# A gated quantized MLP: conditioning by VectorE, another order of the first slots, and five steps in other places

## The chip, the core and the metric

One core of a Trainium2 chip runs the kernel. Its engines work side by side, each through its own list of instructions in order, and wait for each other by semaphores: TensorE (PE in the profile, its weight loads PEld), VectorE (DVE), ScalarE (ACT), GpSimd (POOL) and SyncE (SP), which here issues nearly all transfers between memory and the on-chip buffers. The metric is the device time of one execution in microseconds, the median of several.

## The reference

x is (4, 1024, 512): four batches of 1024 tokens. Each batch has a row of 128 conditioning values, which scales the 512 channels after an RMS norm. Then comes a gated product with 2048 values and 2048 gates, an exact GELU, and a product down to 512 with both sides quantized: 8 bits for each token, three levels for the weights.

```python
scale = cond @ norm_w.T + 1.0
ms = jnp.mean(x * x, axis=-1, keepdims=True)
h = x * (scale[:, None, :] * jax.lax.rsqrt(ms + EPS))
u = h @ up_w.T
val, gate = jnp.split(u, 2, axis=-1)
h = val * jax.nn.gelu(gate, approximate=False)
hq = act_quant(h)          # round(h * 127 / max|h|) of each token, scaled back
wq = weight_quant(down_w)  # -1, 0, 1 by the mean of |w|
y = hq @ wq.T + x
```

## The kernel before

**Slots.** The 2048 values and gates are cut into 16 tiles of 128, and each batch into two halves of 512 tokens. One tile for one batch is a *slot*; g counts slots over all batches (slot 16 is the first of the second batch), j within a batch. A float32 number is carried as two 16-bit parts, a *high* and a *low* one, so each product has three terms: low by high, high by low, high by high.

**The first batch** (`first_batch` and the straight code above it) is computed plainly: `plain_half(j, h)` makes, for tile j and half h, 12 matmuls for the gate (`pg`), a Gelu on ACT, 12 matmuls for the value (`pv`) and a DVE operation that multiplies them into H. Meanwhile the up weights are prepared: `w_load` (SP), `w_range` (DVE finds each row's power of two), `w_scale` (POOL), `w_turn` (PE turns the tile), `w_high` (ACT casts the high part), `w_low` (DVE the rest), `w_evac` (ACT copies the turned tile), `s_sums` (POOL makes sums of quarters), `s_high` (ACT), `s_low` (POOL) and `s_spill` (SP writes them to memory). The later batches load these sums and need 7 products of 6 matmuls for a slot instead of 8 (`product`, `slot`).

**Conditioning.** norm_w is loaded first on SP (L157), then x. PE turns cond and norm_w (`cond_prep`), multiplies them (`cond_scale`, L172), and the largest value of each batch gives a power of two that is spread over all partitions (`cond_largest`, `cond_range`). `first_high` and `first_low` multiply the turned x of batch 0 by scT while they cast it. For the other batches `cond_rows` multiplies all rows out, each 32 times, and writes them to `rows_dram`; `cond_load_scale` fetches one (`sc`) with four transfers, and `cond_bring` (L217) scales it on DVE.

**Down weights.** `d_load`, then `d_sum` on ACT for the absolute values, `d_total` (DVE, L350, makes `wpart`) and `d_mean` (PE's `pmean`, L355, and two DVE operations), all in slot 5; `d_round` and `d_put` prepare wd. ACT's `d_sum` writes into a buffer that DVE's largest values (`pair_max`, tile gm) also use.

**Order.** The program order of each engine is written out by hand. Pools of buffers make a writer wait for the last reader; of PSUM banks A and E have two, B one, po three. In the later batches a slot's steps have places x, y and z: `plan` gives the four token tiles of the next batch their places for load, norm, scale, high, low and turn; the rest is filled in by cost.

**The end.** The last batch has no slot behind it. Eight tiles of the batch before (`old_tile`) run on PE while DVE and ACT quantize the last batch (`work`), `per` steps of work between two tiles; `ends` holds the evacuations of tiles that still wait for it. Then come the last products (`po_end`), whose banks the old tiles hold.

Of the kernel before, what the change touches and what calls it, by code (L numbers as in the profile page):

```python
# [41 lines left out]
def glu_quant_kernel(  # L42
# [22 lines left out]
    G = P // B  # L65
# [37 lines left out]
    rows_dram = tc.dram_tile([P, D], F32, name="rows_dram")  # L103
# [42 lines left out]
    condT = cpool.tile([P, B], F32, name="condT")  # L146
# [4 lines left out]
    nwT = R[:, 1, 512:1024]  # L151
    cg = R[:, 1, 1024:1152].rearrange("p (b o) -> p b o", b=B)
    junk = R[:, 1, 2048:4096].rearrange("p (n d) -> p n d", d=D)
    cn = sm.tile([B, C], F32, name="cn", bufs=1)

    def cond_load():
        SP.dma_start(out=nw, in_=norm_w.rearrange("(k p) c -> p k c", p=P))  # L157
        ACT.dma_start(out=cn, in_=cond)

    def cond_prep():  # L160
        pc = bank("E", 2, [P, B], "pc")
        PE.transpose(pc, cn, ident[:B, :B])
        DVE.tensor_copy(condT, pc)
        pt = bank("E", 2, [P, D], "pt")
        for k in range(NK):
            PE.transpose(pt[:, k * P : (k + 1) * P], nw[:, k, :], ident)
        ACT.copy(nwT, pt)

    def cond_scale():
        pq = bank("A", 2, [P, NK, B], "pq")  # L170
        for k in range(NK):
            PE.matmul(pq[:, k, :], nwT[:, k * P : (k + 1) * P], condT, start=True, stop=True)  # L172
        DVE.tensor_scalar(scT, pq, 1.0, None, ALU.add)

    def cond_largest():
        mx = sm.tile([P, B], F32, name="mx", bufs=1)
        DVE.tensor_reduce(
            mx, scT.rearrange("p k b -> p b k"), AX.X, ALU.max, apply_absolute_value=True
        )
        pm = bank("A", 2, [B, P], "pm")  # L180
        PE.transpose(pm, mx, ident)
        return pm

    def cond_range(pm):
        d4 = sm.tile([B, 1], F32, name="d4", bufs=1)
        DVE.tensor_reduce(d4, pm, AX.X, ALU.max)
        DVE.tensor_scalar(d4, d4, 1e-30, None, ALU.max)
        pow2_floor(d4)
        dg = sm.tile([B, B], F32, name="dg", bufs=1)
        DVE.tensor_scalar(dg, ident[:B, :B], d4, 1.0 / X_UP, ALU.mult, ALU.mult)  # L190
        pd = bank("A", 2, [P, B], "pd")
        PE.matmul(pd, ones[:B, :], dg, start=True, stop=True)
        DVE.tensor_copy(dx, pd)
    def cond_bring_first():
        DVE.reciprocal(ux, dx)
        DVE.tensor_scalar(scT[:, :, 0], scT[:, :, 0], ux[:, 0:1], None, ALU.mult)

    def cond_rows():

        pq = bank("A", 2, name="pq_rows")  # L200
        PE.matmul(pq, cg.rearrange("p b o -> p (b o)"), nwT, start=True, stop=True)
        rows = junk[:, 0]
        DVE.tensor_scalar(rows, pq, 1.0, None, ALU.add)
        SP.dma_start(out=rows_dram, in_=rows)

    def cond_groups():
        DVE.tensor_copy(cg, condT.rearrange("p (b o) -> p b o", o=1).to_broadcast([P, B, G]))

    def cond_load_scale(b):

        sc = wpool.tile([P, D], F32, name=f"sc_{b}", tag="sc", bufs=1)
        for n in range(P // G):
            SP.dma_start(out=sc[n * G : (n + 1) * G, :], in_=rows_dram[b * G : (b + 1) * G, :])
        return sc
# [15 lines left out]
    def wf(j):  # L230

        return H[:, 15 + j % 2].rearrange("p t (n f) -> p (t n) f", n=2)
# [3 lines left out]
    def w_load(j):  # L236
        for t in (1, 0):
            SP.dma_start(out=wn(j)[:, t], in_=up_v[j][:, t])
# [254 lines left out]
    def h_half(g, h):  # L493
        return h_slots(g)[:, 0, h]
# [13 lines left out]

    live = {}

    def slot(g, x=nothing, y=nothing, z=nothing, middle=nothing, late=nothing):

        up = g < B * NJ
        prev = live.pop(g - 1, None)
        if up:
            cur = live[g] = {}
            cur["A"] = bank("A", 2, name=f"A_{g}")
            product(0, g, cur["A"], True, True)
            pb = bank("B", 1, name=f"B_{g}")
            ACT.copy(pb, cur["A"])  # L520
            cur["E"] = bank("E", 2, name=f"E_{g}")
            product(4, g, cur["E"], True, True)
            cur["v"] = wpool.tile([P, TOK], F32, name=f"v_{g}", tag="v")
            ACT.copy(cur["v"], cur["E"])  # L524
            product(1, g, pb, False, True)
            cur["t1"] = wpool.tile([P, TOK], F32, name=f"t1_{g}", tag="t1")
            ACT.activation(cur["t1"], pb, AF.Gelu, scale=gain(g, 1))  # L527
# [6 lines left out]
        if up:  # L534
            product(5, g, cur["A"], False, True)
            cur["t2"] = wpool.tile([P, TOK], F32, name=f"t2_{g}", tag="t2")
            ACT.copy(cur["t2"], cur["A"])  # L537
# [122 lines left out]
    DVE.memset(eps, EPS)  # L660
    ACT.activation(start_t, one, AF.Sqrt)
# [13 lines left out]
    def first_sums(n):  # L675
        ACT.activation(junk[:, n % 4], X0[:, n], AF.Square, accum_out=ssq0[:, n : n + 1])
        DVE.scalar_tensor_tensor(
            junk[:, (n + 1) % 4], X0[:, n + 1], 1.0, X0[:, n + 1], ALU.mult, ALU.mult,
            accum_out=ssq0[:, n + 1 : n + 2],
        )  # L680

    def rsqrt_start(t, y):

        z = sm.tile([P, NA], F32, name="newton", bufs=1)
        ACT.activation(z, t, AF.Sqrt, scale=1.0 / D, bias=eps)
        DVE.tensor_scalar(t, t, 1.0 / D, EPS, ALU.mult, ALU.add)
        DVE.reciprocal(y, z)
        DVE.tensor_tensor(z, y, y, ALU.mult)
        DVE.scalar_tensor_tensor(z, z, -0.5, t, ALU.mult, ALU.mult)
        DVE.scalar_tensor_tensor(y, z, 1.5, y, ALU.add, ALU.mult)  # L690
# [17 lines left out]
    def first_low(h, k, pt):  # L708
        c = slice(h * TOK, (h + 1) * TOK)
        DVE.scalar_tensor_tensor(  # L710
            XP[:, 1, k, c], pt, scT[:, k, 0:1], XP[:, 0, k, c], ALU.mult, ALU.subtract
        )
# [7 lines left out]
    cond_load()  # L720
    first_load(0)
    first_load(2)
    w_load(0)
    first_load(4)
    w_load(1)
    first_load(6)
    w_load(2)
    keep_warm(6)
    cond_prep()
    for n in (0, 2):  # L730
        first_sums(n)
    rsqrt_start(ssq0[:, 0:4], rs0[:, 0:4])
    cond_scale()
    keep_warm(3)
    pm = cond_largest()
    first_scale(0, ACT)
    first_scale(1, DVE)
    first_scale(2, ACT)
    first_scale(3, ACT)
    ptx = [po_bank(f"ptx_0_{k}") for k in range(3)] + [bank("A", 2, name="ptx_0_3")]  # L740
    first_turn(0, ptx)
    first_turn(1, ptx)
    w_range(0, 1, 2)
    w_scale(0, (1,), ACT)
    cond_range(pm)
    first_turn(2, ptx)
    first_turn(3, ptx)
    w_turn(0, [bank("E", 2, name=f"pw_0_{t}") for t in (1, 0)], (1,))
    cond_bring_first()
    first_high(0, 0, ptx[0])  # L750
# [4 lines left out]
    first_low(0, 0, ptx[0])  # L755
    w_low(0, (1,))
    for k in range(1, NK):
        first_high(0, k, ptx[k])
        first_low(0, k, ptx[k])
    w_turn(0, ts=(0,))  # L760
    w_high(0, (0,))
    w_evac(0)
    w_low(0, (0,))
    ACT.activation(start_t, neghalf[:, 0:1], AF.Gelu)
    w_range(1)
    w_gain(1)
    cond_groups()
    w_scale(1)
    for n in (4, 6):
        first_sums(n)  # L770
    rsqrt(ssq0[:, 4:8], rs0[:, 4:8])
    plain_half(0, 0)
    w_turn(1)
    w_high(1)
    w_evac(1)
    w_low(1)
    for n in range(4, 8):
        first_scale(n, ACT if n % 2 else POOL)
    w_load(3)
    w_range(2)  # L780
    w_gain(2)
    w_scale(2)
    plain_half(1, 0)
    ptx = [po_bank(f"ptx_1_{k}") for k in range(3)] + [bank("A", 2, name="ptx_1_3")]
    for n in range(NA, 2 * NA):
        first_turn(n, ptx)
    for k in range(NK):
        first_high(1, k, ptx[k])
        first_low(1, k, ptx[k])
    s_sums(0)  # L790
    w_load(4)
    w_range(3)
    w_gain(3)
    w_scale(3)
    plain_half(0, 1)
    w_turn(2)
    w_high(2)
    w_low(2)
    w_range(4)
    w_gain(4)  # L800
    s_high(0)
    s_low(0, POOL)
    s_spill(0)
    w_evac(2)
    s_sums(1)
# [13 lines left out]
    def first_batch(j, sc):  # L819
# [23 lines left out]
        if j == 5:  # L843
            d_mean(part)
# [13 lines left out]
        plain_half(j, 1)  # L858
        for i, h in pairs[2:]:
            for f in pair_max(0, i, h):  # L860
                f()
# [18 lines left out]

    for n in D_LOAD[0] + D_LOAD[1]:
        d_load(n)
    w_load(5)
    cond_rows()
    plain_half(1, 1)
    s_high(1)
    s_low(1, POOL)
    s_spill(1)
    w_turn(3)
    w_high(3)  # L890
    w_low(3)
    w_evac(3)
    w_scale(4)
    s_sums(2)
    s_high(2)
    s_low(2, POOL)
    s_spill(2)
    for n in D_SUM[1]:
        d_sum(n)
    for j in range(2, NJ):  # L900
        if j == 4:
            sc = cond_load_scale(1)
            cond_bring(1, sc)
        first_batch(j, sc if j >= 4 else None)
# [72 lines left out]
    for b in range(1, B):  # L977
# [18 lines left out]
        if b + 1 < B:  # L996
# [8 lines left out]
                (p0 + 2, p0 + 4, ((9, "z"), (12, "x"), (12, "y"), (13, "z"), (14, "x"), (14, "y"))),  # L1005
# [130 lines left out]
    per = -(-len(work) // (2 * NA - 3))  # L1136
# [12 lines left out]
    for f in ends[:1] + work + ends[1:]:  # L1149
        f()  # L1150
# [48 lines left out]
```

## Time and profile before

| | |
|---|---|
| runs | 765.2 us median of three, 761.91 to 765.37 |
| profiled execution | 766.27 us; span from first to last instruction 764.5 us |
| granted clock | 0.997 |
| 0 to 5 us, 5 to 10 us | PE busy 3.57 and 3.58, transfers 161 and 342 GB/s |
| 50 to 60, 60 to 70 us | transfer share 0.99 and 1.01 |
| 100 to 150, 150 to 200 us | PE 50.00 and 50.00, DVE 44.11 and 41.11, POOL 36.98 and 43.07 |
| sc from rows_dram | four issues 71.81 to 74.86, used on DVE at 78.92 |
| dq from am_dram, 1024 single elements | 4.2 to 4.4 us from issue to landing |

Busy times are sums over an engine's instructions; PE's are pipelined and their ends modelled, so a busy PE is not one at its peak. A wait is put down to the engine whose semaphore came last. Idle time costs only where it delays the chain that ends last.

### The profile page before, as it was taken

What the parts mean: (1) busy time and instruction counts of PE and PEld (TensorE: products, weight loads), DVE (VectorE), ACT (ScalarE), POOL (GpSimd) and SP (SyncE); (2) the same over time, 40 slices, a digit from 0 to 9 for tenths busy, and PEclk for the clock granted to TensorE, in tenths of its full rate; (3) what the DMA queues carried; (4) which work ended last, traced back from release to release, by engine and by line L of the source; (5) the groups of instructions that cost most, each with busy time, mean ns of one, the idle gap of its engine ahead of it and who ended that gap; (6) DMA issues with size and microseconds to landing.
All of it is one profiled execution on the core that took longest, in us unless ns stands there. A gap on an engine that the chain in (4) does not pass through costs nothing.

```text
span 764.5 us, 9577 instructions
## 1 busy us (share of the span) xinstructions
PE 744.8 (97%) x3485; PEld 347.6 (45%) x3485; DVE 544.0 (71%) x781; ACT 376.0 (49%) x614; POOL 199.4 (26%) x221
## 2 busy tenths in 40 slices
PE   7899899999999999999999999999999999999997
PEld 4454445545444444444444444444444444444443
DVE  5746769988879886544679886554679887445895
ACT  4558445566234656353434666444333665332263
POOL 0478547989310030333010020243020000000100
PEclk9999999999999999999999999999999999999999
DMA  6159355778823325366833334557732333333153
GB/s 224 38 187 380 108 172 150 196 191 194 232 90 115 116 81 174 136 185 180 193 110 102 112 117 136 175 154 202 179 119 97 97 102 112 115 106 110 51 185 110
DMA packets 92784, 111.54 MB, mean 146 GB/s; under 512 B 59961, under 2 KB 60477, under 8 KB 92738
## 3 DMA queue, kind: packets, MB, share of 16 engines
q1 hardware_dynamic: 92730, 110.94, 47.8%
q8 instruction: 27, 0.44, 0.2%
q14 instruction: 19, 0.16, 0.1%
q10 hardware_dynamic: 8, 0.00, 0.0%
HBM read 74.47 MB, written 23.35 MB: 128 GB/s over the span
## 4 chain that ended last, share of the span: by engine, by line
PE 87%; DMA 3%; DVE 3%; ACT 2%; SPq 1%; issue 1%; POOL 1%; DVEq 0%; ACTq 0%; POOLq 0%
PE A L464 32%; PE E L464 16%; PE po L646 10%; PE B L464 8%; PE pv L479 8%; PE pg L479 8%; PE po_end L646 3%; PE pw L267 1%; DMA s_dram<-SXY 1%; DMA H<-in_x_dram 1%; PE ptx L702 1%; DVE gm L565 1%; DMA sc<-rows_dram 1%; DMA R<-in_x_dram 1%; DVE R L567 1%
## 5 line engine op out<-in xcount | busy, mean ns | idle before, releaser
L464 PEld LDWEIGHTS <-SXY 128*128 128x128 f16 x2016 | 197.2, 98 | 241.8 <-issue 4.2
L464 PE MATMUL A<-R,SXY 128*128 128x512 f16 x1152 | 264.6, 379 | 1.0 <-ACT t L537 1.0
L464 PE MATMUL E<-R,SXY 128*128 128x512 f16 x576 | 140.0, 379 | 0.0
L530 DVE SCALAR_TENSOR_TENSOR H<-A,sg,t 128x512 f32<-128x512 f32 x48 | 36.0, 750 | 83.5 <-PE A L464 83.5
L543 ACT ACTIVATE t<-t,sg 128x512 f32<-128x512 f32 x48 | 34.5, 720 | 106.5 <-DVE t L542 106.5
L646 PE MATMUL po<-wd,R 128*128 128x512 bf16 x384 | 85.3, 379 | 0.0
L646 PEld LDWEIGHTS <-R 128*128 128x128 bf16 x512 | 50.1, 98 | 61.5 <-issue 1.2
L620 DVE TENSOR_TENSOR H<-H,am 128x1024 f32<-128x1024 f32 x64 | 76.3, 1217 | 0.0
L581 POOL PARTITION_ALL_REDUCE am<-R x8 | 14.6, 1819 | 223.7 <-DVE R L567 223.7
L464 PE MATMUL B<-R,SXY 128*128 128x512 f16 x288 | 70.0, 379 | 2.4 <-ACT B L520 2.4
L565 DVE TENSOR_REDUCE gm<-H 128x512 f32<-128x1024 f32 x56 | 69.0, 1233 | 2.6 <-DMA wd<-tn 1.6
L542 DVE TENSOR_TENSOR t<-E,t 128x512 f32<-128x512 f32 x48 | 32.6, 680 | 49.4 <-PE E L464 49.4
L479 PE MATMUL pg<-R,SXY 128*128 128x512 f16 x264 | 61.7, 379 | 3.0 <-ACT R L706 1.7
L479 PE MATMUL pv<-R 128*128 128x512 f16 x252 | 63.2, 379 | 0.0
L373 POOL TENSOR_TENSOR rs<-ssq,neghalf 128x2 f32<-128x2 f32 (+1 forms) x13 | 9.6, 738 | 205.5 <-DVE ssq L372 205.2
L479 PEld LDWEIGHTS <-SXY 128*128 128x128 f16 x396 | 38.6, 98 | 49.2 <-issue 3.6
L479 PEld LDWEIGHTS <-R 128*128 128x128 f16 x372 | 36.6, 99 | 43.4 <-issue 1.0
L527 ACT ACTIVATE t<-B,sg 128x512 f32<-128x512 f32 x48 | 33.0, 687 | 38.8 <-PE B L464 37.0
L537 ACT COPY t<-A 128x512 f32<-128x512 f32 x48 | 28.0, 583 | 47.8 <-PE A L464 47.7
L628 ACT ACTIVATE H<-H 128x1024 f32<-128x1024 f32 x39 | 40.9, 1049 | 20.9 <-DVE H L620 20.9
L567 DVE TENSOR_TENSOR R<-R,gm 128x512 f32<-128x512 f32 x56 | 42.9, 766 | 1.4
L524 ACT COPY v<-E 128x512 f32<-128x512 f32 x48 | 28.1, 585 | 31.2 <-PE E L464 26.9
(154 smaller groups left out, 884.9 us busy)
## 6 DMA issues: line engine op xcount, KB each, us to landing
SXY<-s_dram SPq DMA_DIRECT2D x48, 640.0 KB, 4.0
SXY<-s_dram SPq DMA_DIRECT2D x48, 256.0 KB, 4.3
s_dram<-SXY SPq DMA_DIRECT2D x11, 896.0 KB, 4.0
H<-in_L_cond_up_w_dram SPq DMA_DIRECT2D x32, 256.0 KB, 4.3
xr<-in_x_dram SPq DMA_DIRECT2D x19, 256.0 KB, 4.7
out_dram<-xr SPq DMA_DIRECT2D x19, 256.0 KB, 2.2
s_dram<-R SPq DMA_DIRECT2D x5, 896.0 KB, 4.7
H<-in_x_dram SPq DMA_DIRECT2D x8, 512.0 KB, 5.8
```

Source lines behind the costliest of these rows:

```text
L464: PE.matmul(o, s[:, w, k, :], tv[:, :, c, l, k, :], start=start and n == 0, stop=stop and n == len(TERMS) - 1, skip_group_check=True,)
L479: PE.matmul(ps, a[k // 2][:, w, k % 2, :], XP[:, l, k, h * TOK : (h + 1) * TOK], start=n == 0, stop=n == len(terms) - 1,)
L524: ACT.copy(cur["v"], cur["E"])
L527: ACT.activation(cur["t1"], pb, AF.Gelu, scale=gain(g, 1))
L530: DVE.scalar_tensor_tensor(h_half(g - 1, 0), prev["A"], gain(g - 1, 0), prev["t1"], ALU.mult, ALU.mult)
L542: DVE.tensor_tensor(prev["t2"], prev["E"], prev["t2"], ALU.add)
L543: ACT.activation(prev["t2"], prev["t2"], AF.Gelu, scale=gain(g - 1, 1))
L565: DVE.tensor_reduce(gm[0], v, AX.X, ALU.max, apply_absolute_value=True)
L567: return [largest, lambda: DVE.tensor_tensor(m, m, gm[0], ALU.max)]
L620: DVE.tensor_tensor(v, v, r.to_broadcast([P, 2, TOK]), ALU.mult)
L628: ACT.activation(v, v, AF.Copy, bias=MAGIC)
L646: PE.matmul(po, q[:, h, j, a * P : (a + 1) * P], wd[:, j, :], start=j == 0, stop=j == NJ - 1,)
```

## The change

The conditioning is computed by DVE: products of norm_w with the broadcast row of cond, summed along the row (`cond_scale` for batch 0, `cond_scale_rest` for the others later). norm_w and cond come over ACT's queue, x first on SP. The range and spread are computed once for batch 0 and once for batches 1 to 3. `cond_rows` writes the three rows from scT, one element for each partition and group, in slot 3; `cond_load_scale` broadcasts a row with one transfer. The start works by tiles of x: the first sums and the Newton steps for two tiles at a time, twelve warming matmuls first, more of them between.

Slots 0 to 2 run on the first 512 tokens; then the second half of x is turned, and the slots run on the second half. `plain_first` is tile 0 with its terms in another order, and the turning of weights between them.

Five steps stand elsewhere: `d_mean` behind the second half of slot 5; in slot 16 the sixth product and its copy ahead of the second product (`first_value`); token 3's high, low and turn one place later each; three steps of work between old tiles; the last work behind all evacuations.

```diff
-    def cond_load():
-        SP.dma_start(out=nw, in_=norm_w.rearrange("(k p) c -> p k c", p=P))
-        ACT.dma_start(out=cn, in_=cond)
...
+    def cond_load(b0, b1):
+
+        v = cond[b0:b1].rearrange("b c -> (b c)").partition_broadcast(P)
+        ACT.dma_start(out=cb[:, b0:b1].rearrange("p b c -> p (b c)"), in_=v)
+
+    def cond_scale(b):
         for k in range(NK):
-            PE.matmul(pq[:, k, :], nwT[:, k * P : (k + 1) * P], condT, start=True, stop=True)
-        DVE.tensor_scalar(scT, pq, 1.0, None, ALU.add)
+            DVE.scalar_tensor_tensor(
+                dots, nw[:, k], 1.0, cb[:, b], ALU.mult, ALU.mult, accum_out=scT[:, k, b : b + 1]
+            )
+
+    def cond_scale_rest():
...
+        DVE.tensor_tensor(v, w, s, ALU.mult)
+        DVE.tensor_reduce(scT[:, :, 1:].rearrange("p k b -> p b k"), v, AX.X, ALU.add)
...
     def cond_rows():
 
-        pq = bank("A", 2, name="pq_rows")
-        PE.matmul(pq, cg.rearrange("p b o -> p (b o)"), nwT, start=True, stop=True)
-        rows = junk[:, 0]
-        DVE.tensor_scalar(rows, pq, 1.0, None, ALU.add)
-        SP.dma_start(out=rows_dram, in_=rows)
+        for b in range(1, B):
+            SP.dma_start(out=rows_dram[b].rearrange("(k p) -> p k", p=P), in_=scT[:, :, b])
...
         sc = wpool.tile([P, D], F32, name=f"sc_{b}", tag="sc", bufs=1)
-        for n in range(P // G):
-            SP.dma_start(out=sc[n * G : (n + 1) * G, :], in_=rows_dram[b * G : (b + 1) * G, :])
+        SP.dma_start(out=sc, in_=rows_dram[b].partition_broadcast(P))
...
+    def plain_first(between):
+
+        ps = {1: bank("B", 1, name="pg_0_0"), 0: bank("A", 2, name="pv_0_0")}
+        gate, a21, a22 = a_parts(0)
+        for n, (t, w, l) in enumerate(
+            ((1, 0, 0), (1, 1, 0), (0, 0, 0), (0, 1, 0), (1, 0, 1), (0, 0, 1))
+        ):
+            if n in between:
+                between[n]()
...
+        def first_value():
+            product(5, g, cur["A"], False, True)
+            cur["t2"] = wpool.tile([P, TOK], F32, name=f"t2_{g}", tag="t2")
+            ACT.copy(cur["t2"], cur["A"])
...
             ACT.copy(cur["v"], cur["E"])
+            if not prev:
+                first_value()
             product(1, g, pb, False, True)
...
-    cond_load()
     first_load(0)
+    w_load(0, (1,))
     first_load(2)
-    w_load(0)
+    w_load(0, (0,))
+    w_load(1)
     first_load(4)
-    w_load(1)
     first_load(6)
     w_load(2)
-    keep_warm(6)
...
+    keep_warm(12)
+    first_sum(0)
+    first_sum(1)
+    cond_scale(0)
+    mx = cond_largest(0, 1)
+    pm = cond_over(mx, 0, 1, "A")
+    rsqrt_start(ssq0[:, 0:2], rs0[:, 0:2])
     keep_warm(3)
-    pm = cond_largest()
+    pd = cond_spread(cond_range(pm, 0, 1), 0, 1, "A")
+    keep_warm(1)
+    first_sum(2)
     first_scale(0, ACT)
+    first_sum(3)
+    w_range(0, 1, 2)
     first_scale(1, DVE)
+    rsqrt_start(ssq0[:, 2:4], rs0[:, 2:4])
+    w_scale(0, (1,), ACT)
     first_scale(2, ACT)
+    cond_undo(pd, 0, 1)
+    cond_bring_first()
+    first_scale(3, DVE)
...
     first_turn(0, ptx)
+    keep_warm(2)
     first_turn(1, ptx)
...
-        if j == 5:
-            d_mean(part)
+        if j == 3:
+            pd = cond_spread(dg, 1, B, "po")
+            cond_undo(pd, 1, B)
+            cond_rows()
...
         plain_half(j, 1)
+        if j == 5:
+            d_mean(part)
...
+    plain_first({1: second_part, 4: second_slot})
+    w_load(3)
...
+    plain_half(1, 0, third_slot)
...
+    plain_half(2, 0, other_half)
+    w_load(5)
+    w_scale(3)
+    s_all(0)
+    s_sums(1)
...
+    cond_scale_rest()
+    mx = cond_largest(1, B)
+    plain_half(0, 1)
+    s_all(1)
+    s_sums(2)
...
+    w_scale(4)
+    plain_half(1, 1)
...
-    for j in range(2, NJ):
+    for j in range(3, NJ):
...
-                (p0 + 2, p0 + 4, ((9, "z"), (12, "x"), (12, "y"), (13, "z"), (14, "x"), (14, "y"))),
+                (p0 + 2, p0 + 4, ((9, "z"), (12, "x"), (12, "y"), (14, "x"), (14, "y"), (14, "z"))),
...
-    per = -(-len(work) // (2 * NA - 3))
+    per = 3
...
-    for f in ends[:1] + work + ends[1:]:
+    for f in ends + work:
         f()
```

## The prediction

> **What bounds the kernel now.** I read the busy row and the chain of waits first: PE is busy for 97% of the span and holds 87% of the chain, so only time in which PE stands, or runs at half its clock, can be won. The list of PE's waits then says where, and the timelines say why. The first 100 us (first rows) and the rest of the span:
>
> ```profile
> PE 744.8 (97%) x3485; PEld 347.6 (45%) x3485; DVE 544.0 (71%) x781; ACT 376.0 (49%) x614; POOL 199.4 (26%) x221
> ...
> PE pmean L355 <- DVE wpart L350: 3.5, 1, 3.5
> PE pm L181 <- DVE mx L177: 1.9, 1, 1.9
> PE pg L479 <- ACT R L706: 1.7, 7, 0.4
> ...
> PE pw L267 <- POOL H L259: 1.1, 2, 0.7
> PE pg L479 <- DVE SXY L289: 1.1, 1, 1.1
> ...
> PE B L464 <- ACT B L520: 2.4, 2, 1.2
> PE A L464 <- ACT t L537: 1.0, 1, 1.0
> ...
> PE po_end L646 <- DVE SXY L653: 0.9, 1, 0.9
> ```
>
> Columns: who waits for whom; us in total, times, longest. Next, rows of the timelines of PE, DVE and ACT (start, length, engine, line, in brackets the idle time before and who ended it) and, between them, the row 90 to 100 of the table by stage, whose last three numbers are granted clock, transfer share and GB/s:
>
> ```profile
> 17.34 0.39 PE L479 MATMUL pg<-R,SXY 128*128 128x512 f16 x1 [0.24 <-ACT SXY L280]
> ...
> 78.92 0.49 DVE L217 TENSOR_SCALAR sc<-sc,ux 128x512 f32<-128x512 f32 x1 [6.19 <-DMA sc<-rows_dram]
> ...
> 91.38 0.42 PE L355 MATMUL pmean<-wpart,one 128*128 128x1 f32 x2 [3.45 <-DVE wpart L350]
> 91.66 1.95 PE L267 MATMUL pw<-ident,H 128*128 128x128 f32 x8
> ...
> 90.00:100.00 10.00, 8.62 (x38) 4.85 (x39) 3.72 (x13) 4.23 (x9) 6.40 (x8) 0.83 0.51 167
> ...
> 215.09 0.69 ACT L527 ACTIVATE t<-B,sg 128x512 f32<-128x512 f32 x1 [1.78 <-DVE sg L488]
> 216.30 2.75 PE L464 MATMUL A<-R,SXY 128*128 128x512 f16 x12 [1.02 <-ACT t L537]
> 364.61 1.85 ACT L443 CAST H<-H 128x512 f16<-128x512 f32 x3
> 366.37 0.57 ACT L520 COPY B<-A 128x512 f32<-128x512 f32 x1
> ```
>
> The reader sees five places: a start in which the first real matmul stands at 17.34; a chopped stretch up to 60.12, where the sixth half slot ends; a stand of 3.45 us at 88 to 91, after which the granted clock of ten microseconds is 0.83 (1.7 us lost; the same eight transposes take 1.95 us there and 1.04 elsewhere); three single waits in batches 1 and 2; one at the end.
>
> **Pace of PE.** A half slot is 24 matmuls: the rows that start at 54.94 and 60.12 give 5.18. Eight transposes take 0.87 (48.01 to 48.89). From 17.34 to 60.12 are 42.78 us; the work in it is 6 x 5.18 + 4 x 0.87 (w_turn) + 1.75 (16 turns of x, at 32.48) + 0.86 (the product for the rows, 41.97 to 42.83) = 37.2, so 5.6 are lost.
>
> **The start, step by step.** Gone: the transposes of the conditioning, its four products, the ACT copy; x no longer queues behind norm_w. Before, the first pair of x tiles was issued at 1.23 and its sums began at 7.29. Now it is issued half a microsecond earlier, but norm_w shares the same transfer engines from ACT's queue: between 6.3 and 7.3, I take 6.8. The second pair has half a weight tile ahead of it (256 KB at about 0.37 MB/us is 0.7 us): 8.9, instead of 8.7. ACT now takes both first sums (2 x 0.72), and Sqrt 0.3: 8.6. DVE's four dot products of 128 elements have no row; between 0.18 (the smallest operations) and 0.69 (512 elements), I take 0.4 with the accumulator read, so 1.6, and 0.4 to add one and take the largest: done at 9.0. Then in DVE's order, by the rows of before: Newton 0.87, range of the conditioning 0.87, range of the gate weights 1.16, scale of tile 1 0.48, second Newton 0.87, spread undone 0.55, scale of tile 3 0.48. That is 9.0 + 5.3 = 14.3, with DVE never idle. A trap is here: the fourth bank of the first turn is the one that holds the spread factor, so PE's first turn ends only when DVE has copied it (13.3); 2 warming matmuls, three turns and the gate weights' turn follow, 2.2 us at full clock. ACT's first high part then runs at 15.5 and **the first matmul at 16.1**, 1.2 earlier than now.
>
> Here a rule decides a size. The Trainium skill, "TensorE: Matmul & The Clock Gate", section "Part 1: The HAM clock gate", says the clock is doubled after one busy window of about 3.4 us, which runs free of the program, and halved after one idle window. The rows show the halving (3.45 us idle, then 0.83). They show the early state by spacing: the six warming matmuls take 2.74 us for what later takes 1.46, so the first 16 us are at half clock. Twelve in place of six, 0.43 apart, are busy for 5.2 us, which holds a whole window in (5.2 - 3.4)/3.4, about half, of all phases, a little more if a nearly full one counts; three, one and two more keep the later windows from being idle. By the rule the clock is full at 13 us, by the row (half until 16) the same turns cost 2.2 more and the first matmuls too. I take full clock, and keep the other as a rival.
>
> **Slots 0 to 2.** The load of the other three conditioning rows costs ACT half a microsecond of issue ahead of the value weights' cast, which DVE does not yet wait for. PE now has three half slots of other weights before it needs the second half of x. Still lost: 1.1 us for the first four matmuls, each behind an ACT high part (0.58 apart against 0.22). The other waits go, since weights and sums come a half slot sooner; but POOL becomes late: its sums (2.8 per slot) and low parts (2.25) stand ahead of the scaling of tile 4. PE ends (2,0) at 16.1 + 3 x 5.18 + 5 x 0.43 + 1.75 + 1.1 = 36.7 and wants tile 4 two halves and a w_turn later, at 47.9; POOL gets the first s_high at 37.1 and needs 2.25 + 2.8 + 2.25 + 2.8 + 1.36: 48.5. So 0.6 is lost. PE's work is 37.2 - 0.86 + 0.43 (half of the first turn, now after the first matmul) = 36.8, and the sixth half ends at 16.1 + 36.8 + 1.1 + 0.6 = 54.6: **5.5 won** with the start. DVE's new product and sum for the other three batches (1536 elements; 1.22 per 1024 by L620, so 3.6 for both) and 0.4 more lie beside the matmuls of half slot (0,1); without that cover they would delay only the release of a bank that has another half slot's time. The two small matmuls for the three batches cost PE 0.2.
>
> **d_mean half a slot later.** It moves past 12 + 12 matmuls and one w_turn on PE (6.05 us), and its two DVE operations behind w_low and one evacuation; behind them on DVE stands only d_round, first needed at 100. wpart is late because DVE stood 6.19 for sc, then worked 12.2 us to wpart. If DVE comes no earlier, PE reaches it 2.6 us after wpart. **3.45 + 1.7 = 5.15 won**, if sc comes no later. sc: its four issues took 3.05 us of SP and are one now. But the rows are written only in slot 3, as 3 x 512 single elements, and sc waits on SP for the first of them, behind the spill of slot 4. The skill, "DMA: Bandwidth & Descriptors", section "Rules for kernel authors", says a strided last dimension becomes one descriptor per element and should be rearranged: 1536 descriptors against 128. The nearest row is dq, 1024 single elements, which lands in 4.3 us, no more than larger transfers. The skill's rule says avoid, the row says 4 to 5 us, once. I take the row. On SP the rows now stand behind four spills and the loads up to slot 7; POOL's pace lets SP issue them near 61, sc at about 66 behind the spill, landed at 70.5. PE ends (4,0) at 71 and (5,1) at 88 (54.6 + 5.2 per half and 0.9 per w_turn). DVE has wpart 12.2 after sc, 83. Slack 5 us. Bounds: nothing lost, or, were each element 0.2 us, 96 per transfer engine, 19 us.
>
> **Single moves.** In slot 16 first_value goes ahead of the Gelu that waits for sg behind pair maxima: the ACT copy of A no longer stands behind it. 1.0 won. Token 3's high part (1.85 on ACT) leaves 13 z, where it stood ahead of the copy of B, for 14 x, behind the Gelu and ahead of a copy that is due 1.8 us later; its low follows on DVE at the same point of the slot as now, its transpose is SP's next issue as now (372.6), 10 us before the batch that reads it: 2 x 1.2 = 2.4 won. At the end three steps between old tiles in place of five let DVE evacuate tile 5 (733.3) seven steps sooner; DVE is full to 752 either way, and PE's last products need its pieces later than they come: 0.9 won, 0 if DVE's order holds up something I don't see.
>
> **Sum.** 5.5 + 5.15 + 1.0 + 2.4 + 0.9 - 0.2 = 14.8. The profiled execution took 766.27 (span 764.5): 751.5. The median shown is 765.2, one microsecond below it, which I don't take off.
>
> **Rivals.** (1) *The start gives nothing*: the clock is half until about 17, x or the dot products come a microsecond late; the sixth half ends 3.4 to 5.4 later than 54.6, as now or little better, and the rest holds: 755 to 757, say 755.5. For it: DVE is a closed chain from 9 to 25 us, so each late step passes on. Against: the waits for POOL and DVE in slots 1 and 2 are gone from the order itself, whatever the first matmul's time. (2) *Only the moves that are named work and sc comes late*: with 8 us more, DVE frees the bank of (4,0) at 81.7, when PE wants it at 79.6, and is a little behind at d_mean too: 2 to 4 us and perhaps the clock, 754 to 757. For it: transfers were saturated at 50 to 70 us (share 0.99 to 1.01). (3) *Slower*: single-element writes to memory at 0.2 us or more each: with 0.25, sc is 24 us late and DVE stands for it, the weight range and the evacuation of (4,0) queued behind; PE stands 18 us for that bank in slot 5 and loses 1.7 of clock: 771.5. It decides from about 0.2 us per element. Against it: dq's 4.3 us. (4) *No change*: DVE or POOL, with less idle time, hands the waits back in slots 6 to 15. Against: there PE stands not at all between 100 and 210, and DVE waited for PE for 8 us.
>
> **Chances.** Likeliest 0.60 (its own range 748 to 755); (1) 0.23; (2) 0.06; (3) and other losses 0.07; (4) 0.04. Range 747.5 to 758.5. 0.5% (3.8 us) is about what a measurement here tells from none. Faster 0.89, within 0.04, slower 0.07.
>
> **What would show it.** First matmul near 16 and sixth half near 54.6; no wait for wpart, and granted clock 1.00 from 90 to 100; waits for t at slot 16 and for B gone; DVE's wait for sc under 5 us. Wrong if a wait for sc, for scaled weights or for a transposed tile of the next batch appears in PE's list with more than 2 us, or a clock below 1.00 past 20 us.

## The result, and the profile after

The changed kernel takes 762.28 us (median of 20 runs, 759.69 to 764.5) where the kernel before, beside it, takes 764.99 (median of 20): ratio 0.9966, 95% interval 0.9954 to 0.9978, or 2.7 us less. 14.8 were forecast. The profiled execution took 763.18, with a span of 761.4. In its list of PE's waits (who waits for whom; us in total, times, longest), whole:

```profile
PE pm L185 <- DVE mx L178: 4.0, 1, 4.0
PE pv L485 <- DVE H L513: 3.4, 1, 3.4
PE pw L273 <- DVE SXY L295: 2.8, 1, 2.8
PE pw L273 <- POOL H L265: 1.8, 1, 1.8
PE pz L752 <- DVE eps L692: 1.4, 1, 1.4
PE pg L527 <- ACT R L740: 0.6, 3, 0.2
PE pg L485 <- ACT g L532: 0.2, 1, 0.2
PE A L470 <- DMA SXY<-s_dram: 0.2, 1, 0.2
PE pz L752 <- DVE dx L205: 0.2, 1, 0.2
```

The waits of slot 16, of both B copies and of the end are gone, and so is the one for `wpart`. New are 3.4 for an evacuation and 2.8 for a low part. The timelines of PE, SP and DVE place them (start, length, engine, line; in brackets the idle time before and who ended it):

```profile
1.43 4.18 PE L752 MATMUL pz<-H 128*128 128x512 f16 x12 [1.43 <-DVE eps L692]
9.64 0.37 PE L185 MATMUL pm<-ident,mx 128*1 128x128 f32 x1 [4.03 <-DVE mx L178]
18.05 0.38 PE L527 MATMUL pg<-R,SXY 128*128 128x512 f16 x1
...
52.17 1.32 PE L273 MATMUL pw<-ident,H 128*128 128x128 f32 x8 [1.76 <-POOL H L265]
...
66.17 2.41 SPq L214 DMA_DIRECT2D rows_dram<-scT  x3
69.45 0.33 SPq L324 DMA_DIRECT2D s_dram<-SXY  x1
79.48 0.33 SPq L219 DMA_DIRECT2D sc<-rows_dram  x1
84.63 0.48 DVE L223 TENSOR_SCALAR sc<-sc,ux 128x512 f32<-128x512 f32 x1 [13.30 <-DMA sc<-rows_dram]
87.75 2.75 PE L485 MATMUL pv<-R 128*128 128x512 f16 x12 [3.45 <-DVE H L513]
93.78 1.09 PE L273 MATMUL pw<-ident,H 128*128 128x128 f32 x4 [2.84 <-DVE SXY L295]
```

The reader sees two losses. **The start:** the first matmul stands at 18.05, behind a PE that stood 4.03 us; the sixth half slot ends at 58.5 (before 60.12, forecast 54.6). **Slot 5:** SP issues the three row writes at 66.17 and can issue the load of `sc` only at 79.48, 13.3 us later. DVE stands 13.30 us for it (6.19 before), and PE then waits for DVE twice, with half clock behind the second wait.

The table by stage, last three numbers granted clock, transfer share and GB/s, shows both. The first four rows are the start, the last is the stretch in which the row writes drain:

```profile
1.40:4.30 2.90, 2.87 (x7) 1.04 (x8) 1.46 (x9) 1.49 (x2) 0.00 (x0) 1.00 0.67 230
4.30:7.70 3.40, 1.31 (x6) 0.39 (x4) 0.00 (x0) 1.63 (x5) 0.00 (x0) 1.00 0.72 227
7.70:17.90 10.20, 8.03 (x29) 5.58 (x30) 8.47 (x41) 4.96 (x10) 0.00 (x0) 0.50 0.70 259
18.00:20.00 2.00, 1.34 (x4) 0.43 (x4) 1.90 (x6) 1.74 (x4) 0.59 (x1) 1.00 0.45 135
...
71.00:80.00 9.00, 9.00 (x47) 4.57 (x46) 0.34 (x1) 4.61 (x11) 1.21 (x2) 1.00 1.07 62
```

The 1.00 of the first row is no measurement, since the profile's record of the clock begins at 4.3 us; the spacing tells it: seven warming matmuls in 2.87 us there, 0.41 each, six in 1.31, 0.22 each, in the next row. So PE came to full clock at 4.3 us, stood for most of 4.3 to 7.7 (busy 1.31 of 3.40) and had half the clock for the next 10.2. From 71 to 80 the transfer engines are busy on paper (1.07) and move 62 GB/s.

### The profile page after: what moved, and what is told of

Same layout as the page of the kernel before. It is cut to its first block, busy times and chain, and to the rows that moved or that the text cites. A ratio compares the mean times of both kernels' runs of the same rounds, so it can differ in the third digit from the quotient of the medians.

```text
span 761.4 us, 9575 instructions
## 1 busy us (share of the span) xinstructions
PE 742.7 (98%) x3482; PEld 346.1 (45%) x3482; DVE 554.1 (73%) x800; ACT 376.7 (49%) x618; POOL 199.0 (26%) x218
## 4 chain that ended last, share of the span: by engine, by line
PE 90%; DMA 4%; DVE 2%; ACT 1%; POOL 1%; issue 0%; SPq 0%; ACTq 0%; DVEq 0%; POOLq 0%
PE A L470 32%; PE E L470 16%; PE po L678 11%; PE pg L485 9%; PE pv L485 8%; PE B L470 8%; PE po_end L678 4%; DMA rows_dram<-scT 2%; PE pw L273 2%; DMA R<-in_cond_dram 1%; POOL SXY L321 1%; DMA SXY<-s_dram 1%; DMA sc<-rows_dram 1%; ACT R L740 1%; PE ptx L736 0%
## 5 line engine op out<-in xcount | busy, mean ns | idle before, releaser
L485 PE MATMUL pv<-R 128*128 128x512 f16 x246 | 61.6, 379 | 3.4 <-DVE H L513 3.4
L485 PE MATMUL pg<-R,SXY 128*128 128x512 f16 x252 | 57.8, 379 | 0.2 <-ACT g L532 0.2
```

Of the source, the lines that this page charges most:

```text
L485: PE.matmul(ps, a[k // 2][:, w, k % 2, :], XP[:, l, k, h * TOK : (h + 1) * TOK], start=n == 0, stop=n == len(terms) - 1,)
```

## The experiments

All ratios are to the kernel before, run beside it on the same chip (its median was 764.99 beside the changed kernel and 765.9 to 766.3 beside the others); intervals are 95%. Kernels that were measured on different chips are compared by their ratios.

| kernel | us | ratio |
|---|---|---|
| before, four single moves | 760.6 | 0.9932 (0.9919 to 0.9946) |
| before, all five moves | 755.7 | 0.9866 (0.985 to 0.9883) |
| changed | 762.28 | 0.9966 (0.9954 to 0.9978) |
| changed, d_mean back | 769.01 | 1.0032 (1.0023 to 1.0042) |
| changed, rows written early | 765.5 | 0.9994 (0.9986 to 1.0003) |
| changed, one row in slot 3 | 762.37 | 0.9955 (0.9939 to 0.9972) |
| changed, rows as 512 bytes | 757.68 | 0.9892 (0.9877 to 0.9908) |
| the same, turned earlier | 757.24 | 0.9884 (0.9866 to 0.9903) |
| ... and rest of the products late | 762.84 | 0.9954 (0.9936 to 0.9972) |
| ... and more warming | 756.11 | 0.9867 (0.9847 to 0.9887) |
| ... and the row spread by PE | 754.0 | 0.9837 (0.982 to 0.9854) |
| ... and the rest on PE | 752.41 | 0.9814 (0.98 to 0.9828) |

### What the five moves are worth by themselves

The kernel before, with four moves (all but d_mean), and with five:

```diff
+            if not prev:
+                first_value()
             product(1, g, pb, False, True)
...
-                (p0 + 2, p0 + 4, ((9, "z"), (12, "x"), (12, "y"), (13, "z"), (14, "x"), (14, "y"))),
+                (p0 + 2, p0 + 4, ((9, "z"), (12, "x"), (12, "y"), (14, "x"), (14, "y"), (14, "z"))),
...
-    per = -(-len(work) // (2 * NA - 3))
+    per = 3
...
-    for f in ends[:1] + work + ends[1:]:
+    for f in ends + work:
```

> The kernel before with four of the five single moves alone (first value of slot 16, token 3 one place later, three steps beside each old tile at the end, the last old tile ahead of the remaining work). By the sum on record 1.0 + 2.4 + 0.9 = 4.3 us less than before: 760.7. Rival (the moves only win in the trace of the changed kernel, because its slots 5 to 15 ran differently): 1 us or less, 764 or more.

> The kernel before with all five single moves, d_mean behind the second half slot of slot 5 among them, and the conditioning and slots 0 to 2 as they were. By the sum on record another 5.15 (3.45 of PE's stand, 1.7 of half clock) less than with four moves: 755.5. Rival (VectorE's wait for sc, 6.2 us before, takes the place of the wait for d_mean, as in the changed kernel): 758.5 to 760.7, with a wait of PE for H in slot 5.

Measured: 5.2 us less with four (4.1 to 6.2), 10.2 with five (9.0 to 11.5), so d_mean brings about 5 more. With five moves no wait for `wpart` is left and `pmean` runs at 93.8 without a stand. Both sums hold. It follows that the rest of the change, conditioning on DVE and the new order of slots 0 to 2, *costs* about 7.6 us (10.2 less 2.6; each of the two has an interval of a microsecond to either side).

### d_mean put back in the changed kernel

```diff
         plain_half(j, 0)
+        if j == 5:
+            d_mean(part)
...
         plain_half(j, 1)
-        if j == 5:
-            d_mean(part)
```

> The changed kernel as it is, with d_mean's matmul put back behind the first half slot of slot 5. If the wait for sc is what stops PE in slot 5, d_mean's move brings nothing there: VectorE reaches wpart behind sc either way, and the time is within 1 us of the changed kernel. If the move still bears: 3 to 5 us more than the changed kernel, 766 or more.

This expectation was a miss: 769.01, ratio 1.0032 against 0.9966, about 5 us more. I had thought that the wait for sc leaves the move nothing. PE's waits in this run, first two rows:

```profile
PE pmean L361 <- DVE wpart L356: 4.9, 1, 4.9
PE pv L485 <- DVE H L513: 4.2, 1, 4.2
```

DVE makes `wpart` behind everything else that waited for sc, so PE waits for it besides the evacuation. The move earns its 5 us in the changed kernel too; something else takes more than that away.

### The row writes: place or form

Early, as they are (behind half slot (0,1), 20 us sooner):

```diff
     plain_half(0, 1)
+    cond_rows()
     s_all(1)
...
             cond_undo(pd, 1, B)
-            cond_rows()
```

> The changed kernel with its three row writes (single 4-byte elements, as they are) issued right behind the first half slot (0,1), some 20 us earlier, as soon as VectorE has the rows. Theory A (the element writes, put behind loads in slot 3, land sc late; VectorE stands before L223 for 13.3 us and cannot read out slot 5): VectorE's wait for sc falls to 6 us or less, PE's waits for H (3.45) and SXY (2.84) and the half clock at 93 go, 8.0 us less: about 754.3 us. Rival A2 (VectorE and POOL are too full in slots 3 to 5, whatever sc does): the waits in slot 5 stay, 762 us. Rival A3 (the writes cost the same wherever they are, and only hit something else): the wait moves to the transfers of slots 0 to 2 that follow, 758 to 762.

In their place, as 16 rows of 512 bytes:

```diff
-        for b in range(1, B):
-            SP.dma_start(out=rows_dram[b].rearrange("(k p) -> p k", p=P), in_=scT[:, :, b])
+        DVE.tensor_copy(scB, scT.rearrange("p k b -> p b k"))
+        pr = po_bank("pr", [B * NK, P])
+        PE.transpose(pr, scB.rearrange("p b k -> p (b k)"), ident)
+        DVE.tensor_copy(rowsT, pr)
+        SP.dma_start(out=rows_dram.rearrange("b (k p) -> (b k) p", p=P), in_=rowsT)
```

> The changed kernel with the rows written at the same place in slot 3, but as 16 rows of 512 bytes: VectorE copies the 16 columns, PE turns them once, VectorE copies the turned rows out (some 0.6 us of VectorE in all). Theory A, with the elements as the cause: the rows land 3 to 5 us after they are issued instead of 13.3, the wait for sc falls under 6 us, the waits of slot 5 go: about 754 us. Rival A4 (the place behind the loads of slot 3 is the cause, and not the size of the pieces): the rows still land 10 us or more after issue, 760 to 762.

Early, the writes cost more than late: 765.5, slower than every case on record had it, and by the ratios some 2 us above the changed kernel. The table by stage of that run, after the writes were issued at 46 to 49:

```profile
53.00:56.00 3.00, 3.00 (x9) 1.07 (x8) 1.82 (x4) 0.28 (x2) 3.00 (x5) 0.50 2.00 58
56.00:59.00 3.00, 3.00 (x15) 1.31 (x14) 0.00 (x0) 0.00 (x0) 2.29 (x4) 0.94 0.63 19
59.00:62.00 3.00, 3.00 (x16) 1.38 (x15) 0.00 (x0) 0.00 (x0) 0.00 (x0) 1.00 0.54 31
```

For nine microseconds hardly a byte moves (58, 19, 31 GB/s), and from 59 on DVE, ACT and POOL all stand. The chain of waits of this run names the spill behind the writes, and the list of waits what it costs:

```profile
49.29 16.89 DMA s_dram<-SXY
```

```profile
PE pd L201 <- DVE dg L195: 6.8, 1, 6.8
```

With pieces of 512 bytes and at the same place, SP and DVE run:

```profile
66.97 0.34 SPq L219 DMA_DIRECT2D rows_dram<-rowsT  x1
72.44 0.32 SPq L224 DMA_DIRECT2D sc<-rows_dram  x1
76.51 0.48 DVE L228 TENSOR_SCALAR sc<-sc,ux 128x512 f32<-128x512 f32 x1 [2.97 <-DMA sc<-rows_dram]
```

The rows land within 5.5 us, DVE has sc 8.1 us sooner than in the changed kernel, no wait is left in slot 5, and the time falls by 0.74%, some 5.7 us. It stays short of the 754 expected, since PE now stands 2.0 for the packed columns. So it is the form, and not the place in slot 3. Turning the rows beside the largest values instead takes that stand from 2.0 to 0.7:

```diff
     mx = cond_largest(1, B)
+    cond_pack()
...
     pm = cond_over(mx, 1, B, "po")
+    cond_turn()
```

> The changed kernel with the rows written as 16 rows of 512 bytes, as in the run that did this within slot 3, but the 16 columns packed by VectorE right behind their largest values and turned by PE beside the turn of those, so that PE does not wait 2.0 us for them in slot 3. That run stood 8.3 us under the kernel before. Theory A (the element writes were what was lost in slot 5, and the 2.0 us what its cure cost): 10 us under the kernel before, about 755.7 where that takes 765.9; no wait of PE over 0.5 us between 55 and 105 us. Rival (PE's 2.0 us of wait is handed to the next step, POOL or VectorE being late anyway): 757 to 758.

757.24: no better than the 757.68 within the intervals, and short of 755.7; the rival's number came. In its profile the clock is 0.83 between 50 and 60, behind a 1.74 us wait for POOL; in this profile what was saved went there. In the profile of the kernel that packs them in slot 3, a wait of 1.75 us at the same step left the clock at 1.00, so the length of the wait alone does not decide it.

### What it is about the form

One row in slot 3, the other two in slot 10:

```diff
-        for b in range(1, B):
+        for b in range(b0, b1):
...
+            cond_rows(1, 2)
+        if j == 10:
+            cond_rows(2, B)
```

> The changed kernel, but only the row of batch 1 is written in slot 3 (512 single elements); the rows of batches 2 and 3 are written in the same way in slot 10. Theory A with a price per element: 1536 elements took 8 us from their first packets to landing (some 5.3 ns each) behind 5 us of loads, so 512 take 2.7 us, the wait for sc falls from 13.3 to about 8 us, at most 1 us of PE's 6.3 us of waits in slot 5 is left: 755 to 758. Rival (a fixed cost of such a transfer, whatever the number of its pieces): sc comes as late as in the changed kernel, 762 to 764. Second rival (the two rows in slot 10 hold up what is needed there): slot 5 is free of waits, but a new wait of 3 to 6 us appears behind slot 10, 760 or more.

762.37, as the first rival had it: a third of the elements, and SP could issue the load of sc at 80.56, even later than 79.48. A price per element is out. The two rows in slot 10 hold up transfers as well (50 GB/s from 160 to 170), but PE waits only 0.54 us there: the writes cost time only where somebody waits for what they delay. Four more kernels, one run each, put one further write behind the rows of the kernel with turned rows and differ in nothing else:

```diff
+            SP.dma_start(out=more_dram.rearrange("(k p) -> p k", p=P), in_=scT[:, :, 1])   # 512 close
+            SP.dma_start(out=more_dram[:, :, 0], in_=scT[:, :, 1])                         # 512 apart
+            SP.dma_start(out=more_dram.rearrange("(p o) -> p o", o=1), in_=scT[:, 0, 1:2]) # 128 close
+            SP.dma_start(out=more_dram, in_=scB[:, 1, :])                                  # 128 of 16 bytes
```

> The kernel with the turned rows, and behind its row write in slot 3 one more write that nobody reads: 512 single elements side by side, as the row of batch 1 in the changed kernel. Control: lands some 13 us after issue by the run with one row (14 there), the spill behind it is held up, a few us of wait for sc.

> As the control, but each of the 512 elements goes to a place 512 bytes from the next. If writes [...]are what queue up: lands 5 to 6 us after issue, as the loads ahead of it allow. If the number of pieces or their size is what costs: 12 to 14 us, as the control.

> As the control, with 128 elements (512 bytes in all) instead of 512. If the cost is one per transfer, whatever its pieces: 12 to 14 us, as the control. If it comes from the pieces that one row of memory takes one after the other: some 8 us less 3/4, that is 7 us after issue.

> As the control, with the same 2 KB in 128 pieces of 16 bytes. If the number of pieces into one place decides: as 128 elements. If the bytes decide: as the control, 12 to 14 us.

The row 72 to 80 of the table by stage, for 512 close, then for 512 apart:

```profile
72.00:80.00 8.00, 8.00 (x43) 4.11 (x41) 0.24 (x1) 3.83 (x8) 0.10 (x1) 1.00 0.85 36
```

```profile
72.00:80.00 8.00, 8.00 (x42) 4.14 (x41) 3.13 (x9) 3.83 (x8) 0.69 (x3) 1.00 0.54 167
```

| write added | time | GB/s, 72 to 80 | the spill behind it, us from issue to landing | DVE waits for sc |
|---|---|---|---|---|
| none | 757.24, median of five on another chip | 200 | 4.9 | 4.26 us |
| 512 elements side by side | 762.74 | 36 | 13.5 | 11.82 |
| 512 elements, 512 bytes apart | 756.14 | 167 | 5.0 | 4.70 |
| 128 elements side by side | 758.52 | 83 | 11.4 | 9.13 |
| 128 pieces of 16 bytes, side by side | 756.13 | 143 | 6.2 | 3.59 |

What costs is single elements *side by side* in memory: the same number of pieces of the same size, spread out, costs nothing that shows. Nor does the same 2 KB in pieces of 16 bytes, which neither case on record had; they delay the spill by 1.3 us and the time not. (Of 128 side by side the time shows little, since sc had slack, but PE waits 2.3 us for a low part again.) The times are single runs; the reading rests on the transfers, which differ by far more. These writes hold up whatever is queued behind them, and 512 of them also what was issued just before: SP, which waits for the rows before it loads sc, could do so at 78.51, though it had issued them half a microsecond ahead of the added write; without the added write it was 72.95, from an issue 0.8 us later. The trace does not show what in the memory makes them wait for each other, and the runs do not part the size of a piece from the number of pieces that fall close together; both stay open.

### The start

30 warming matmuls in place of 12, and 6 in place of 3 behind the first turn; then also the conditioning row as one row of 512 bytes, spread by PE (there 12, the spread and 8 in place of 30):

```diff
-    keep_warm(12)
+    keep_warm(30)
...
-    keep_warm(3)
+    keep_warm(6)
```

```diff
-    cond_load(0, 1)
+    cn = rowsT[0:1, :]
+    ACT.dma_start(out=cn, in_=cond[0:1])
...
+    pcb = bank("B", 1, [P, C], "pcb")
+    PE.matmul(pcb, ones[:1, :], cn, start=True, stop=True)
...
-                dots, nw[:, k], 1.0, cb[:, b], ALU.mult, ALU.mult, accum_out=scT[:, k, b : b + 1]
+                dots, nw[:, k], 1.0, pcb, ALU.mult, ALU.mult, accum_out=scT[:, k, b : b + 1]
```

> The kernel with the turned rows (run beside this), with 30 warming matmuls in place of 12 and 6 in place of 3 behind the first turn, so that PE is busy until VectorE has the largest value at 9.6 us. Theory B (PE's stand of 4 us behind the 12 warming matmuls halved the clock at 7.7 us): the granted clock stays 1.00 from about 4.3 us on, 128-wide turns take 0.11 us each in place of 0.25, the first matmul of the first half slot starts at about 16.0 in place of 18.05, and the time falls by 1.5 to 2 us. Rival (the start is bound by VectorE, ScalarE and the x transfers, PE at half clock keeps up): 0.5 us or less. Second rival (the gain is handed back before slot 3, by POOL's scaling of tile 4): first matmul earlier, PE's wait for POOL longer by as much, time the same.

> As the run with more warming, and the conditioning row of batch 0 read as one row of 512 bytes and spread over the partitions by one PE matmul, in place of a transfer to 128 partitions that landed at 7.8 us. If that broadcast is what VectorE's dots waited for: dots from about 6.2 us, largest value at 7.8 in place of 9.6, and if it also held up the second pair of x rows, those land by 8 us in place of 9.15: first matmul 1 to 2 us earlier than with more warming alone, and the time with it. Rival (the row lands no earlier, or the second x pair, ScalarE and the weights set the first half slot): 0.5 us or less.

With more warming the same two stretches as above read:

```profile
4.30:7.70 3.40, 3.40 (x16) 1.48 (x15) 0.00 (x0) 1.63 (x5) 0.00 (x0) 1.00 0.68 228
7.70:17.90 10.20, 8.14 (x45) 4.52 (x44) 9.13 (x41) 6.61 (x13) 0.00 (x0) 1.00 0.79 288
```

The clock stays full, as expected; the first matmul starts at 16.4 (18.05 in the changed kernel, 17.15 in the profile of the turned rows, whose clock came back earlier). 1.1 us in the medians, where 1.5 to 2 were expected, and the two intervals overlap, so the gain is shown in the profile and not by the times. With the row on PE, DVE's dots start at 6.09 in place of 7.89 and the first matmul at 14.47; the time is 754.0, 2.1 us less, as expected.

### POOL and tile 4

The products for batches 1 to 3 moved from 40 us to ahead of half slot (2,1). A load has overwritten their inputs by then, so the rows of these batches hold other values in this kernel; and VectorE waits for that load before it starts.

```diff
-    cond_scale_rest()
-    mx = cond_largest(1, B)
-    cond_pack()
     plain_half(0, 1)
...
     w_low(4)
+    cond_scale_rest()
+    mx = cond_largest(1, B)
+    cond_pack()
     plain_half(2, 1)
```

> The kernel with the turned rows, with the products for batches 1 to 3 on VectorE (4.2 us) not beside POOL's s_low(0) at 40 us, but ahead of the half slot (2,1). Theory C (VectorE's large product slows POOL's s_low(0) from 2.3 to 3.8 us, and that is PE's 1.8 us of wait for the scaling of tile 4): s_low(0) takes 2.3 us, the wait is 0.3 us, the time 1.5 us less. Rival (POOL has too much to do before tile 4, whoever runs beside it): the wait stays above 1 us. Second rival (VectorE, now later, makes PE wait for the largest values or for an H half instead): a wait of PE for DVE of 1 to 3 us near 55 us, time the same or more.

Both the theory and its second rival show: `s_low(0)` takes 2.27 us in place of 3.79 and the wait for tile 4 falls to 0.2, but PE stands 7.6 us for the largest values, where the rival had 1 to 3. And the `s_low` that now stands beside the product is the one that grows:

```profile
59.27 3.78 POOL L330 TENSOR_TENSOR SXY<-H,SXY 128x768 f16<-128x768 f32 x2 [1.49 <-ACT SXY L326]
```

So the products were given to PE instead:

```diff
+    def rest_turn():
+        pc = po_bank("pc", [P, B])
+        PE.transpose(pc, cn, ident[:B, :B])
+        DVE.tensor_copy(condT, pc)
+        pt = po_bank("pt", [P, D])
+        for k in range(NK):
+            PE.transpose(pt[:, k * P : (k + 1) * P], nw[:, k, :], ident)
+        ACT.copy(junk[:, 0], pt)
+
+    def rest_rows():
+        pq = po_bank("pq", [B, D])
+        PE.matmul(pq, condT, junk[:, 0], start=True, stop=True)
+        DVE.tensor_scalar(junk[:B, 1], pq, 1.0, None, ALU.add)
...
-    plain_half(0, 1)
+    plain_half(0, 1, rest_turn)
...
-    plain_half(1, 1)
+    plain_half(1, 1, rest_rows)
```

> The kernel with warming and the row spread by PE, with the products for batches 1 to 3 taken from VectorE (2.5 + 1.75 us) and given to PE: five turns of the weights and the conditioning between the two matmul groups of (0,1), one 512-wide f32 matmul in (1,1) that leaves the three rows on four partitions, VectorE adds one and takes their largest values there (some 1.3 us); no turn of largest values, rows written as 2 KB each. Theory C (VectorE's large product is what slows POOL before tile 4): s_low(0) 2.3 us in place of 3.8, PE's wait for POOL 1.7 down to 0.3 or less, PE's 1.0 for the turned rows gone, PE busy 1.6 us more: about 1.0 to 1.5 us under the run with warming and the row, 752.5 to 753. Rival (VectorE and POOL are level there, the wait comes back on another tile): the same time or more, a new wait for DVE or ACT between 38 and 62 us.

752.41, the fastest here: 1.9% under the kernel before (interval 1.7 to 2.0), 1.3% under the changed one by their ratios even at the nearest ends of the intervals (0.9828 against 0.9954). All of PE's waits that its profile lists, except those of 0.2:

```profile
PE pz L767 <- DVE eps L707: 1.4, 1, 1.4
PE pz L767 <- DVE dx L207: 1.1, 1, 1.1
PE pg L542 <- ACT R L755: 1.1, 4, 0.4
```

POOL's wait is gone without a new one, although PE does the work of five turns and a product more. Against the kernel with the row spread by PE the intervals overlap, so of this last step the profile shows the gain and the times do not.

## Why the prediction was wrong, by its own steps

**Which step failed.** "The nearest row is dq, 1024 single elements, which lands in 4.3 us [...] I take the row." sc was to land at 70.5 with 5 us of slack; DVE got it at 84.63. Of these 14 us some 5 came ahead of the writes, which SP issued at 66.17 and not near 61; by themselves they cost nothing that shows, since the rows of 512 bytes went out at 66.97, gave DVE sc at 76.51 and left no wait in slot 5. Another 8 are the writes: 13.3 us from their issue to that of the load, where 5 were forecast. dq's row is a *read* of single elements, into the chip; the change adds single-element *writes* to memory, side by side, and no row of the trace before had one. Against it stood the Trainium skill, "DMA: Bandwidth & Descriptors", section "Rules for kernel authors", and its advice, to make the last dimension contiguous, was right, and its cure was worth 5.7 us. But the reason I tied to it, the number of descriptors, was not: 512 single elements 512 bytes apart cost nothing, 128 side by side do. The bound that I kept open, 0.2 us per element, had the wrong form too, since a third of the elements costs the same. By the trace slot 5 lost 8.0 us from this: 3.45, 2.84 and 1.7 of half clock (0.83 from 90 to 100).

**Slots 0 to 2.** 5.5 us were forecast, 1.6 came. Three terms of the sum were mis-sized.
- *Clock full at 13 us.* I priced twelve warming matmuls at 5.2 us of half clock. The clock doubled while they ran, at 4.3, so they ended at 5.61; PE then stood 4.03 us, and the clock was halved until 17.9. The trap is that warming which works shortens itself. More of it kept the clock and brought the first matmul to 16.4, near the forecast 16.1.
- *Dots done at 9.0.* They took 0.33 each and not 0.4, and x landed at 4.8 and not 6.8, but the broadcast of the conditioning row, 6.55 us from issue to landing, had no price in the sum, and DVE waited for it until 7.89; the largest value was there at 9.6.
- *POOL late by 0.6.* 1.76 by the trace: I priced `s_low(0)` at 2.25, as before. It took 3.79, beside DVE's product of 1536 elements, which I had hidden "beside the matmuls" without asking whom else it touches. Away from it, it took 2.27.

The first matmul came 1.95 us late and POOL 1.16 later than forecast; the remaining 0.8 of the 3.9 us no run isolates.

**What was right.** d_mean: 5.15 forecast, about 5 measured, in the kernel before and in the changed one. The single moves: 4.3 forecast, 5.2 (4.1 to 6.2) measured.

**The rivals.** Two came true at once, which no case held: (1), a start that gives nothing or little better, and (2), sc late, by 8 us through the writes alone. Rival (2) named the place rightly, the bank of (4,0), but gave it 2 to 4 us instead of 8. With the measured losses in the sum, 751.5 + 3.9 (58.5 against 54.6) + 8.0 = 763.4; the profiled execution took 763.18. That this comes so close is in part luck, since the single moves alone were worth 0.9 more than their term. Rival (3)'s sum was off by 0.3: 751.5 + 18 + 1.7 is 771.2.

## What to carry to other kernels

Look for the operation that the trace does not have, and price it by a row of the same direction and pattern: a read is no row for a write. A row of 512 numbers that lies across partitions is turned by PE and written in one piece: two small copies and a turn, which here brought sc 8 us sooner and the time down by 5.7. And when an engine's work is called hidden, ask who shares something with it: here a transfer queue, and a neighbour engine.

## What the runs showed of the hardware, unexpected

- Single 4-byte writes side by side in memory held up the transfers of the core for about 8 us, whether 512 or 1536 of them (36 and 62 GB/s meanwhile); 128 lengthened the next spill from 4.9 to 11.4 us. 512 of them spread 512 bytes apart did not (5.0), and 2 KB in 16-byte pieces hardly did (6.2).
- The clock was halved 3.4 us after it had been doubled, behind a stretch in which PE was busy for 1.31 of 3.40, and only 2.1 us into its stand. In the run with turned rows it was halved at 52.8, behind a stand of 1.74 us. The Trainium skill, "TensorE: Matmul & The Clock Gate", section "Part 1: The HAM clock gate", speaks of an idle window of about 3.4 us; here stretches of that length with 39% of work, and with 49% (1.67 of 3.42, 49.39 to 52.81), were enough.
- POOL's `s_low`, two operations on two on-chip inputs each, was longer by 1.5 us while DVE ran a product of 2.46, also on two:

```profile
39.52 3.79 POOL L321 TENSOR_TENSOR SXY<-H,SXY 128x768 f16<-128x768 f32 x2 [1.87 <-ACT SXY L317]
...
46.31 2.28 POOL L321 TENSOR_TENSOR SXY<-H,SXY 128x768 f16<-128x768 f32 x2
```

The Trainium skill, "SBUF — State Buffer", section "SBUF: two separate sides", says that the two engines share a pair of ports which one holds for a whole instruction. The trace agrees, in both directions: the first of the two operations ran at its usual 1.65, and DVE's product, begun under it at 40.32, took 2.46 where 1.8 are an estimate from the 1.22 per 1024 of the kernel before; the second took 2.19 in place of 0.67 and ended 0.5 after the product. The two runs that took the product away gave POOL its 2.27 us back.
